# A decoder layer on one core: the setup loads issued from two queues in turns instead of one

## The chip, the cores and the metric

The kernel runs on one core of a Trainium2 chip. A core has five engines that this text names: PE (TensorE, matmuls and transposes), DVE (VectorE), ACT (ScalarE), POOL (GpSimd) and SP (SyncE, which computes nothing and issues transfers). Each engine works off its own list of instructions, in the order in which the program put them there. A DMA is issued by an instruction in the list of SP or of ACT; the bytes are then moved by 16 DMA engines. The metric is the device time of one execution in microseconds (us); lower is better.

## The reference

The reference is one pre-norm decoder layer in float32 over 128 sequences of 128 tokens with 256 features, 16 heads of 16 features. `_layernorm` has no weights.

```python
x = x + attn(_layernorm(x))                      # self attention, softmax over 128 keys, no mask
x = x + xattn(_layernorm(x), ctx_1024, mask)     # scores where mask == 0 are replaced by 1e-9
x = x + ffn(_layernorm(x))                       # 256 -> 1024 -> 256

def ffn(x):
    h = gelu(x @ absmean(W_fc).T)                # absmean: weights to -1, 0, 1
    return layernorm(h, ln_w, ln_b) @ absmean(W_proj).T

def absmean(W):
    Ws = W / (mean(abs(W)) + 1e-6)
    return sign(Ws) * minimum(round(abs(Ws)), 1)
```

The host only transposes the context and the weights.

## The kernel before, in words

The 128 sequences are worked in 32 groups of four (`G = 4`, 512 tokens). For each group a few streams of steps exist, written as Python generators: `prepare_self` (layer norm, transposes, queries, keys and values of self attention), `attention` (scores, softmax and weighted values of all rows), `prepare_keys` and `prepare_cross` (the same preparation for cross attention), `finish` (the feed-forward part). `constants` and `ternary_weights` run once. The order in which the streams advance is written out by hand: the strings `START`, `ORDER` and `END` hold one letter per step, and `for letter in START + ORDER * (n_groups - 4) + END: next(streams[letter])` (L859) emits the steps. Every engine's list follows that order. Nothing is reordered later; semaphore waits are added by the framework.

Ahead of all streams stands the setup block, L126 to L149. It is emitted first, so whatever it puts into an engine's list stands ahead of that engine's whole work. In this order it loads:

- the four sequences of group 0, `x`, 128 KB each, from SP and ACT in turns (L95), as loads 1 to 4;
- `attn_wq` (load 5), `attn_bq`, `attn_bk`, `attn_wk`, `attn_wv` (load 9), each weight 256 KB, each bias 1 KB, through `load` (L110);
- `ctx_t`, the context of group 0, 512 KB, through `load_context` (L102), load 10;
- `xattn_wk`, `xattn_wv` (loads 11 and 12), `xattn_bk`, `xattn_bq`, `attn_wo`, `attn_bv` (load 16) and `attn_bo`;
- the mask, `unmasked` (L136, load 18), and four copies of it in strips, `rows_32` (L140, loads 19 to 22);
- `xattn_wq`, `xattn_wo`, `xattn_bv`, `xattn_bo` (loads 23 to 26);
- the raw feed-forward weights `raw_w`, 1 MB each (L146, loads 27 and 28);
- `ln_w` and `ln_b` (loads 29 and 30), 4 KB each in 1024 separate elements of 4 bytes.

Only ACT's two loads of `x` are issued by ACT. All the others are issued by SP.

The first work after the setup block is the layer norm of group 0. `statistics` (L274) on DVE reads `x`, `deviation` (L280, L281) on POOL gives `rstd`, `apply` (L285) on DVE and POOL writes `xn`, PE transposes it into `pt` (L303), and ACT copies the two halves of `pt` to `xn_t` in `transposed_copy` (L314). These two copies are ACT's first instructions that compute. Then PE forms the queries `pq` (L323), and ACT writes `qt` from them (L380). `output_bias` (L218 to L221) uses `attn_bv` and `attn_wo`; `masks` (L223) reads the mask tiles; `ternary_weights` (L516) reads the raw weights.

Of the kernel before, what the change touches and what calls it, by code (L numbers as in the profile page):

```python
# [27 lines left out]
P = 128  # L28
# [9 lines left out]
S4 = 4  # L38
# [31 lines left out]
def tile_decoder_layer(ctx: ExitStack, tc: tile.TileContext, a: dict, out: bass.AP):  # L70
    nc = tc.nc
# [17 lines left out]
    def load_group(b):  # L89
        x = p_in.tile([P, G, D], F32, name="x", tag="x")  # L90

        queues = (nc.sync, nc.scalar) if b == 0 else (nc.sync,)
        step = G if b else 1
        for i, j in enumerate(range(0, G, step)):
            queues[i % len(queues)].dma_start(  # L95
                x[:, j : j + step], a["x"][b * G + j : b * G + j + step].rearrange("g s d -> s g d")
            )
        held[b] = x

    def load_context(b):  # L100
        ctx_t = p_in.tile([P, CC, T], F32, name="ctx_t", tag="ctx_t", bufs=1)
        nc.sync.dma_start(ctx_t, a["ctx_t"][:, b * T : (b + 1) * T].rearrange("(c p) t -> p c t", p=P))  # L102
        return ctx_t


    w_self, w_cross = {}, {}

    def load(name, shape, src):
        t = const.tile(shape, F32, name=name)
        nc.sync.dma_start(t, src)  # L110
        return t

    def load_weights(w, pre, names):
        for m in names:
            w[m] = load(f"{pre}_w{m}", [P, CC, D], a[f"{pre}_w{m}_t"].rearrange("(c p) o -> p c o", p=P))

    def load_biases(w, pre, names):
        for m in names:
            w["b" + m] = load(f"{pre}_b{m}", [P, CC], a[f"{pre}_b{m}"].rearrange("(c p) -> p c", p=P))

    def load_output(w, pre):
        load_weights(w, pre, "o")
        load_biases(w, pre, "v")
        w["bo"] = load(f"{pre}_bo", [P, D], a[f"{pre}_bo"][None, :].to_broadcast([P, D]))

    with nc.allow_non_contiguous_dma(reason="a few hundred bias elements, once"):  # L126
        load_group(0)
        load_weights(w_self, "attn", "q")
        load_biases(w_self, "attn", "qk")
        load_weights(w_self, "attn", "kv")  # L130
        context_0 = load_context(0)
        load_weights(w_cross, "xattn", "kv")
        load_biases(w_cross, "xattn", "kq")
        load_output(w_self, "attn")
        unmasked = p_one.tile([P, P], I32, name="unmasked", tag="xn_0")
        nc.sync.dma_start(unmasked, a["mask"])  # L136

        rows_32 = p_one.tile([P, S4, P], I32, name="rows_32", tag="xn_1")
        for r in range(S4):
            nc.sync.dma_start(rows_32[r * 32 : (r + 1) * 32], a["mask"].rearrange("(c i) k -> i c k", c=S4))  # L140
        load_weights(w_cross, "xattn", "q")
        load_output(w_cross, "xattn")
        raw_weights = []
        for src, shape in ((a["w_fc_t"], [P, CC, FF]), (a["w_proj_t"], [P, FC, D])):
            raw = p_one.tile(shape, F32, name="raw_w", tag="g", bufs=2)
            nc.sync.dma_start(raw, src.rearrange("(c p) o -> p c o", p=P))  # L146
            raw_weights.append(raw)
        ln_w = load("ln_w", [P, FC], a["ln_w"].rearrange("(c p) -> p c", p=P))
        ln_b = load("ln_b", [P, FC], a["ln_b"].rearrange("(c p) -> p c", p=P))  # L149
# [755 lines left out]
```

## Time and profile before

| | us |
|---|---|
| median of 3 runs (lowest, highest) | 2740.94 (2736.33, 2741.34) |
| the profiled execution, device time | 2737.08 |
| its span, from the first instruction to the last | 2735.1 |
| PE busy in the span | 2681.2 (98%) |
| ACT busy in the span | 1579.2 (58%) |

The profile is one execution, and its times count from the start of the span. An engine's row in the timeline gives the start, the length and, in square brackets, the idle time ahead of the instruction with what ended that idle time. "SPq" and "ACTq" are the issues of DMAs in the lists of SP and ACT: the length of such a row is how long the issuing engine was held, not how long the bytes travelled. The chain of waits is the work that ended last, followed back through what released each step. The trace also has a record of when the parts of each DMA had landed; the text calls these the completion records.

### The profile page before, as it was taken

The numbers are of one execution on the slowest core, as the hardware profiler recorded it, in microseconds if no ns is written. First come the engines' busy times: TensorE is split into PE (matmuls) and PEld (weight loads), VectorE is DVE, ScalarE is ACT, GpSimd is POOL, SyncE is SP. The second block draws the span as 40 slices with busy tenths as digits, with TensorE's granted clock in tenths as the row PEclk, the third lists the DMA queues.
The fourth block names the chain that finished last, engine by engine and source line by source line (L and its number), as shares of the span: only waits on it lengthen the run. The fifth ranks groups of instructions, "written<-read, shape, count | busy, mean of one in ns | idle before, by whom it ended". The sixth has DMA issues, their size and how long they took to land.

```text
span 2735.1 us, 77049 instructions
## 1 busy us (share of the span) xinstructions
PE 2681.2 (98%) x32845; PEld 1920.3 (70%) x32845; DVE 2118.4 (77%) x3916; ACT 1579.2 (58%) x2508; POOL 1336.5 (49%) x1425
## 2 busy tenths in 40 slices
PE   7999999999999999999999999999999999999998
PEld 4567777677777777776777776777777777777666
DVE  5677787777887777887777877777877778877777
ACT  3455665655665655666556666556656556665446
POOL 2344554544554554554445545445545445545443
PEclk9999999999999999999999999999999999999999
DMA  4121111221121221122211112211112211212210
GB/s 118 33 50 42 42 41 50 57 57 32 45 48 49 57 53 31 42 53 53 58 42 41 42 49 57 58 41 40 44 49 58 58 30 45 49 50 50 50 26 16
DMA packets 110093, 130.28 MB, mean 48 GB/s; under 512 B 32312, under 2 KB 69048, under 8 KB 109752
## 3 DMA queue, kind: packets, MB, share of 16 engines
q1 hardware_dynamic: 109464, 125.11, 18.9%
q8 instruction: 259, 4.24, 0.7%
q14 instruction: 82, 0.67, 0.1%
q10 hardware_dynamic: 288, 0.26, 0.0%
HBM read 71.38 MB, written 18.84 MB: 33 GB/s over the span
## 4 chain that ended last, share of the span: by engine, by line
PE 89%; DVE 7%; issue 2%; ACT 1%; POOL 1%; DMA 0%; DVEq 0%; POOLq 0%; ACTq 0%; SPq 0%
PE st L760 10%; PE av L805 9%; PE pq L323 9%; PE s L699 9%; PE py L500 8%; PE ph L442 8%; PE pk L323 8%; PE po L335 8%; PE pv L335 8%; PE pt L303 3%; PE pg L476 2%; PE s L688 2%; PE st L784 2%; DVE g L487 1%; PE pn L727 1%
## 5 line engine op out<-in xcount | busy, mean ns | idle before, releaser
L710 DVE TENSOR_REDUCE mx<-s 128x8 f32<-128x1024 f32 x512 | 601.0, 1215 | 83.7 <-PE s L699 83.2
L793 ACT ACTIVATE w_t<-st 128x1024 f32<-128x1024 f32 x512 | 496.8, 1022 | 202.6 <-PE st L784 122.0
L280 POOL TENSOR_SCALAR rstd<-agg 128x4 f32<-128x4 f32 (+2 forms) x163 | 39.0, 239 | 965.7 <-DVE agg L275 965.7
L285 POOL TENSOR_SCALAR xn<-x,agg,rstd 128x256 f32<-128x256 f32 x378 | 457.9, 1227 | 9.9
L413 POOL TENSOR_TENSOR o_raw<-o_raw,factors 128x256 f32<-128x256 f32 x252 | 181.4, 748 | 384.8 <-DMA factors<-by_head 279.3
L770 DVE COPY_PREDICATED_SCALAR st<-masked_t,masked_score 128x1024 f32 x256 | 316.1, 1280 | 68.3 <-PE st L760 68.3
L808 ACT COPY raw<-av 128x512 f32<-128x512 f32 x256 | 151.0, 590 | 318.7 <-PE av L805 313.8
L485 ACT ACTIVATE g<-pg,ln_w 128x256 fp32r<-128x256 f32 (+1 forms) x520 | 205.8, 473 | 175.8 <-PE pg L476 163.5
L699 PE MATMUL s<-kt,qt 32*128 32x256 f32 x4096 | 300.0, 403 | 3.2 <-ACT w_t L793 2.2
L500 PE MATMUL py<-w_proj,g 128*128 128x256 f32 x2048 | 279.8, 289 | 1.0 <-DVE g L487 0.6
L805 PE MATMUL av<-w_t,v 128*32 128x128 f32 x8192 | 279.4, 277 | 0.5 <-DVE q_max L732 0.4
L805 PEld LDWEIGHTS av<-w_t,v 128*32 128x32 f32 x8192 | 210.6, 110 | 98.4 <-issue 81.5
L500 PEld LDWEIGHTS py<-w_proj,g 128*128 128x128 f32 x2048 | 254.1, 189 | 12.9 <-issue 1.3
L442 PE MATMUL ph<-w_fc,xn 128*128 128x512 f32 x1024 | 259.4, 403 | 3.4 <-DVE v L371 1.2
L285 POOL TENSOR_SCALAR g<-g,agg,rstd 128x1024 f32<-128x1024 f32 x63 | 241.1, 3827 | 6.6
L487 DVE SCALAR_TENSOR_TENSOR g<-pg,ln_w,g 128x256 fp32r<-128x256 f32 (+1 forms) x520 | 212.5, 469 | 30.3 <-ACT g L485 30.0
L699 PEld LDWEIGHTS s<-kt,qt 32*128 32x128 f32 x4096 | 188.2, 185 | 63.8 <-issue 40.5
L442 PEld LDWEIGHTS ph<-w_fc,xn 128*128 128x128 f32 x1024 | 184.5, 188 | 58.1 <-DVE xn L431 10.3
L760 PEld LDWEIGHTS st<-q_max,kt 32*128 32x128 f32 x4096 | 128.7, 186 | 60.4 <-DVE negm_self L721 42.5
L274 DVE BATCH_NORM_STATS2 stats<-g 128x6 f32<-128x512 f32 x256 | 161.1, 670 | 1.0 <-ACT g L449 1.0
L449 ACT ACTIVATE g<-ph 128x512 f32<-128x512 f32 x256 | 146.6, 599 | 25.3 <-PE ph L442 24.1
L760 PEld LDWEIGHTS st<-qt,kt 32*128 32x128 f32 x4096 | 128.5, 186 | 45.4 <-DVE mx L710 25.0
(130 smaller groups left out, 4615.5 us busy)
## 6 DMA issues: line engine op xcount, KB each, us to landing
o_raw<-raw SPq DMA_DIRECT2D x504, 64.0 KB
factors<-by_head SPq DMA_DIRECT2D x126, 256.0 KB
ctx_t<-in_ctx_t_dram SPq DMA_DIRECT2D x32, 512.0 KB
x<-in_x_dram SPq DMA_DIRECT2D x31, 512.0 KB
out_dram<-x SPq DMA_DIRECT2D x31, 512.0 KB
sums<-raw SPq DMA_DIRECT2D x126, 16.0 KB
by_head<-r SPq DMA_DIRECT2D x63, 32.0 KB
raw_w<-in_w_fc_t_dram SPq DMA_DIRECT2D x1, 1024.0 KB
```

Of the source, the lines that this page charges most:

```text
L285: engine.tensor_scalar(dst[:, j], src[:, j], agg[:, j, 0:1], rstd[:, j : j + 1], ALU.subtract, ALU.mult)
L323: nc.tensor.matmul(out, w[:, c, o * P : (o + 1) * P], src_t[:, c], start=(c == 0), stop=(c == CC - 1))
L335: nc.tensor.matmul(rows[:, j], src_t[:, c, (j0 + j) * P : (j0 + j + 1) * P], w[:, c], start=(c == 0), stop=(c == CC - 1),)
L442: nc.tensor.matmul(ph, xn_parts[i][:, c, (j0 + j - at) * P : (j0 + j - at + 1) * P], w_fc[:, c, n * 512 : (n + 1) * 512], start=((i, c) == ...
L487: nc.vector.scalar_tensor_tensor(parts[1][:, f0 + f, tok], pieces[:, f], scales[f], parts[0][:, f0 + f, tok].bitcast(F32), ALU.mult, ALU.s ...
L500: nc.tensor.matmul(rows[:, j], parts[i][:, f, j * P : (j + 1) * P], w_proj[:, f], start=((i, f) == terms[0]), stop=((i, f) == terms[-1]),)
L699: nc.tensor.matmul(s[r // 2][:, r % 2, 2 * o : 2 * o + 2], qt[strip, o, tok], kt[strip, o, :, tok], start=(stage == "self"), stop=True, sk ...
L710: nc.vector.tensor_reduce(mx[:, 2 * half : 2 * half + 2], s[half], AX.X, ALU.max, negate=True)
L760: nc.tensor.matmul(s[r // 2][:, r % 2, n], kt[strip, n // 2, n % 2, tok], added[strip, n // 2, n % 2] if stage == "self" else qt[strip, n ...
L770: nc.vector.copy_predicated(s[half].rearrange("p r n q -> p (r n) q"), masked_t[:, None, :].to_broadcast([P, 8, P]), masked_score[:, :, No ...
L793: nc.scalar.activation(w_t[:, 2 * half : 2 * half + 2], s[half], AF.Exp)
L805: nc.tensor.matmul(av[32 * r : 32 * r + 32, n], v[:, j, head : head + 32], w_t[:, r, n], start=True, stop=True)
```

## The change

A helper `queue()` turns a list of two queues round at each call and returns the first: ACT at the first call, SP at the second, and so on. `load`, the load of the mask, the four strip loads and the two raw weight loads take their queue from it. The loads of `x` and of the context are as they were. The tiles, the order of the loads in the program and everything after the setup block are the same.

```diff
+    setup_queues = [nc.sync, nc.scalar]
+
+    def queue():
+
+        setup_queues.reverse()
+        return setup_queues[0]
+
     def load(name, shape, src):
         t = const.tile(shape, F32, name=name)
-        nc.sync.dma_start(t, src)
+        queue().dma_start(t, src)
         return t
...
-        nc.sync.dma_start(unmasked, a["mask"])
+        queue().dma_start(unmasked, a["mask"])
...
-            nc.sync.dma_start(rows_32[r * 32 : (r + 1) * 32], a["mask"].rearrange("(c i) k -> i c k", c=S4))
+            queue().dma_start(rows_32[r * 32 : (r + 1) * 32], a["mask"].rearrange("(c i) k -> i c k", c=S4))
...
-            nc.sync.dma_start(raw, src.rearrange("(c p) o -> p c o", p=P))
+            queue().dma_start(raw, src.rearrange("(c p) o -> p c o", p=P))
```

Counted through the program, ACT issues loads 2, 4, 5, 7, 9, 12, 14, 16, 18, 20, 22, 24, 26, 28 and 30, that is two of `x`, `attn_wq`, `attn_bk`, `attn_wv`, `xattn_wv`, `xattn_bq`, `attn_bv`, `unmasked`, the second and fourth strip, `xattn_wo`, `xattn_bo`, the raw projection weights and `ln_b`. SP issues the other fifteen.

## The prediction

> **What bounds the kernel now.** I read the page first: the shares by engine, then the chain that ended last.
>
> ```profile
> span 2735.1 us, 77049 instructions
> PE 2681.2 (98%) x32845; PEld 1920.3 (70%) x32845; DVE 2118.4 (77%) x3916; ACT 1579.2 (58%) x2508; POOL 1336.5 (49%) x1425
> PE 89%; DVE 7%; issue 2%; ACT 1%; POOL 1%; DMA 0%; DVEq 0%; POOLq 0%; ACTq 0%; SPq 0%
> ```
>
> PE is busy 98% of the span and carries 89% of the chain; DMAs carry 0%. So no steady part of the run waits for a load. Whatever the change does, it does in the first tens of microseconds, either by starting PE's stream earlier or by starting it later. The lists are fixed in order, so a shift of that start is carried to the end: nothing later on the chain is tied to the clock time of a setup load.
>
> Next the chain of waits in order of time, for the first 20 us:
>
> ```profile
> 0.72 2.66 DMA x<-in_x_dram
> ...
> 7.19 2.59 POOL xn L285 x2
> 9.78 0.04 issue
> 9.83 1.33 PE pt L303 x5
> 11.16 2.67 PE pq L323 x4
> 13.83 0.86 PE pb L220 x4
> 14.69 1.72 PE pq L323 x4
> 16.41 3.45 PE pk L323 x8
> ```
>
> The only load on it is `x`, which the change leaves alone. From 9.83 us the chain runs on PE without a break until 19.9 us, and through it passes ACT's copy of `pt` to `xn_t`. The timeline of ACT shows what stands in its list ahead of that copy:
>
> ```profile
> 0.72 0.90 ACTq L95 DMA_DIRECT2D x<-in_x_dram  x2
> 1.65 1.28 ACT L314 ACT_TABLE_LOAD   x1 [1.65 <-PEq L893]
> 10.34 0.59 ACT L314 COPY xn_t<-pt 128x512 f32<-128x512 f32 x1 [7.41 <-PE pt L303]
> 11.19 0.59 ACT L314 COPY xn_t<-pt 128x512 f32<-128x512 f32 x1 [0.27 <-PE pt L303]
> ```
>
> Two issues, a table load of 1.28 us that belongs to the copy's line and stands right ahead of it, and then 7.41 us idle. That idle time is all the cover that ACT can offer. Last, the timeline of SP, for what an issue holds the issuer, and SP's own waits:
>
> ```profile
> 8.25 0.47 SPq L110 DMA_DIRECT2D attn_bo<-in_attn_bo_dram  x1
> 10.46 0.34 SPq L136 DMA_DIRECT2D unmasked<-in_mask_dram  x1
> ...
> 15.67 0.47 SPq L146 DMA_DIRECT2D raw_w<-in_w_proj_t_dram  x1
> 16.18 2.60 SPq L110 DMA_DIRECT2D ln_w<-in_ln_w_dram  x1
> 18.83 5.20 SPq L110 DMA_DIRECT2D ln_b<-in_ln_b_dram  x1
> ```
>
> ```profile
> SPq L136 <- DMA ctx_t<-in_ctx_t_dram: 1.7, 1, 1.7
> SPq L140 <- DMA xattn_wk<-in_xattn_wk_t_dram: 0.4, 1, 0.4
> SPq L140 <- DMA xattn_wv<-in_xattn_wv_t_dram: 0.4, 1, 0.4
> ```
>
> The waits are the important lines. `unmasked` needs nothing of `ctx_t`, yet it waited for it; the first two strips waited for `xattn_wk` and `xattn_wv`. Counted through the program, load 18 waited for load 10, 19 for 11, 20 for 12: eight back each time. So the loads share eight completion semaphores in turn, over both queues, and every issue from load 9 on waits until the load eight places earlier has landed. On SP that held nobody. On ACT it would hold the copy at L314.
>
> **The change, part by part.** *What it takes from SP.* Thirteen issues leave SP's list. SP's next use is the `x` of group 1 (issued at 24.07), which DVE first reads at 36.77; after that SP's next issue is at 52.59. Neither is on the chain: worth 0. Bandwidth: the windows view has the DMA engines at a share of 0.78 in 0 to 10 us and 0.75 in 10 to 20 with one queue issuing, and no load but `x` on the chain, so faster landing is worth 0 as well. From below, could anything gain? The longest wait for a setup load, DVE for `attn_bv`, ends at 12.96, and PE only comes to that product (`pb`) at 13.66, directly behind `pq`. No gain.
>
> *What it puts on ACT.* Thirteen more issues, 15 in all, ahead of the table load and the two copies, since the setup block is emitted first. Issue alone costs 0.51 us from start to start (2.11, 2.62, 3.13, 3.65 on SP), so 15 of them end at 0.72 + 15 x 0.51 = 8.4 us if nothing holds them. With the table load, 9.7: still inside the idle time that ends at 10.34. What breaks the cover is the wait for eight back:
>
> - Load 18, `unmasked`, is now on ACT and waits for `ctx_t`. When does that land? Before, 1792 KB came with and ahead of it on one queue, and it landed at 10.45 (completion record; SP went on at 10.46). With two queues served in turns, SP has x, x, `attn_bq`, `attn_wk`, `ctx_t` (1025 KB) and ACT in as many descriptors x, x, `attn_wq`, `attn_bk`, `attn_wv` (769 KB): the same sum. I take 10.5, with 9.5 and 11.5 as bounds. ACT has issued nothing that computes by then.
> - Load 20 (second strip) waits for `xattn_wv`, before at 11.87: issued 11.9. Load 22 waits for `xattn_bq` (12.23): 12.3. Load 24 waits for `attn_bv` (DVE got it at 12.96): 12.9.
> - Load 26, `xattn_bo`, waits for `unmasked`, issued at 10.5. Before, that took from 10.46 to 13.68: 13.7.
> - Load 28, the raw projection weights, waits for load 20; the strip issued at 11.88 before landed at 14.08. ACT itself is free at 13.7 + 0.51. So 14.2.
> - Load 30, `ln_b`, waits for load 22 (landing about 14.3, 2.0 us after issue) and for ACT (14.7). Its own price is the open one. From below it is an ordinary issue, 0.47 us. From above it is `ln_b`'s 5.20. The nearest row is `ln_w`'s 2.60, which also followed the projection weights directly: from the issue of these to the end of `ln_w` it took 18.78 - 15.67 = 3.11 us. I take that: 14.2 + 3.11 = 17.3.
>
> Then the table load: 17.3 + 0.03 + 1.28, and the first copy starts at 18.6 instead of 10.34. Its input has been ready since 10.3. **The chain is late by 8.3 us.**
>
> *Behind the copy.* PE's list is at `pq`; DVE and POOL wait in turn for scores and rows; all of it moves together. Two small terms: the second copy then follows at once (0.5 us behind instead of 0.85), a gain of 0.3; and PE stands idle from about 11.2 to 19. The trace shows one slow stretch early on: the window 25 to 30 us, after PE had been idle, has a granted clock of 0.66, that is 3.4 us at half speed or 1.7 us lost. Whether the longer idle time adds such a stretch is open between 0 and 1.7; I take the middle, 0.8. Together +0.5, and the sum is **+8.8 us**.
>
> The profiled execution took 2737.08, its span 2735.1; the change would make that 2745.9. It lies below the median of the runs (2740.94), whose mean is 2739.5. I set the sum on the mean of the runs: 2739.5 + 8.8 = 2748.3.
>
> *Two rules held against rows.* The Trainium skill, "ScalarE: Activation LUTs", section "What ACT_TABLE_LOAD costs", gives 1283 ns for the load and about 1380 ns more for a drain. The row here has 1.28 us, and late in the run a table load that starts at 2720.57 is followed by an activation at 2721.86, so no drain shows; by the rule the estimate would be 1.4 us higher, 2749.7. The skill's "DMA: Bandwidth & Descriptors", section "Issuing engines are not separate DMA queues", says that issuing from several engines only saves sequencer time, "which is usually small relative to the DMA itself". The rows of 2.60 and 5.20 us for 4 KB speak against "small"; by the rule `ln_b` would cost an ordinary issue and the estimate would be 2746.2.
>
> **The rivals.** *`ln_b` finds room.* ACT's queue then holds only half the loads, so the issue may take 0.47 us: 14.7 + 0.04 + 0.47 = 15.2, copy at 16.5, late by 6.2 + 0.5 = 6.7, 2746.2. For it: less stands in each queue. Against: the 1024 pieces of the projection weights stand directly ahead in the same queue, as they did ahead of `ln_w`.
>
> *`ln_b` pays the full 5.20*, because the two queues hold each other up, or the strips land later: 2.6 more, 11.4 in all, 2750.9. For it: `ln_w` is issued from SP at the same moment. Against: nothing in this trace has two queues busy after 1.7 us.
>
> *ACT's idle time covers all of it; not slower.* If the alternating service brings the early loads home sooner, or the waits do not fall to ACT, its issues end at 8.4 and the table load at 9.7, and the copy starts at 10.34 as before: 2739.5. The point that decides is whether ACT's last issue ends before 9.0 us. Against: it would need `ctx_t` and the strips to land some five us earlier at an unchanged DMA share of 0.75 or more, and the eight-back waits are in the rows. For a real gain there is no place on the chain.
>
> **How the numbers follow.** Forecast 0.60; `ln_b` finds room 0.17; full price 0.15; covered 0.08. About 0.2%, 5.5 us here, is what a measurement of this kernel can tell from no change; against the median the line is at 2746.4. The forecast lies nearly all above it (0.56 of 0.60), the full price wholly (0.15), the cheap `ln_b` just under half (0.07): 0.78 slower. Of what is left, 0.19 is within the bound and 0.03 is faster, from run-to-run spread with the covered case. Range: the low end is the cheap `ln_b` with the runs' spread of 3 us below their mean, 2743; the high end is the full price with the top of the runs' spread and a whole slow stretch of PE (+1.9 and +0.9), 2754. That leaves the covered case and a little on each side outside.
>
> **What would show it.** Right: ACT's timeline has 15 issues, a gap at `unmasked` until about 10.5 us and waits for DMAs at the strips; the table load comes after the last issue, and the first copy starts near 18.6 without waiting for `pt`; the work of PE in the chain is unchanged, with a stretch ahead of it that is ACT's queue. SP's `x` of group 1 is issued several us before 24.07. Wrong: a first copy still at 10.3, a table load still at 1.65, or a copy at 18 us with a span that did not grow, which would mean that the early chain has slack I have not seen.

## The result, and the profile after

| | before | after |
|---|---|---|
| median, us (runs) | 2738.82 (9) | 2747.77 (9) |
| lowest to highest | 2733.58 to 2741.59 | 2743.42 to 2748.55 |
| profiled span | 2735.1 | 2744.9 |

The ratio is 1.0035, with a 95% interval of 1.0027 to 1.0044: slower by about 9 us. The forecast was 2748.3 us.

The page of the changed kernel, its span, the shares by engine and the chain:

```profile
span 2744.9 us, 77048 instructions
PE 2681.9 (98%) x32845; PEld 1920.5 (70%) x32845; DVE 2119.5 (77%) x3916; ACT 1579.1 (58%) x2508; POOL 1337.7 (49%) x1425
PE 89%; DVE 7%; issue 2%; ACT 1%; POOL 1%; DMA 1%; ACTq 0%; DVEq 0%; POOLq 0%; SPq 0%
```

All engines are busy for the same time as before, within 1.2 us (PE 2681.9 against 2681.2). The span grew by 9.8 us, so what was added is waiting. On the page only the DMA share of the chain shows it, 1% instead of 0%. ACT's timeline shows where it lies (an issue's row gives its start and how long ACT was held):

```profile
7.77 0.48 ACTq L143 DMA_DIRECT2D unmasked<-in_mask_dram  x1
9.33 2.35 ACTq L147 DMA_DIRECT2D rows<-in_mask_dram  x2
...
13.24 0.38 ACTq L153 DMA_DIRECT2D raw_w<-in_w_proj_t_dram  x1
16.88 0.38 ACTq L117 DMA_DIRECT2D ln_b<-in_ln_b_dram  x1
17.29 1.28 ACT L321 ACT_TABLE_LOAD   x1 [17.29 <-DMA xattn_bo<-in_xattn_bo_dram]
18.58 1.07 ACT L321 COPY xn_t<-pt 128x512 f32<-128x512 f32 x2
23.04 0.69 ACT L387 ACTIVATE qt<-pq,attn_bqs 128x512 f32<-128x512 f32 x1 [3.38 <-PE pq L330]
```

The first copy of `pt` starts at 18.58 us instead of 10.34, and no wait for PE stands beside it any more: its input had been ready for eight microseconds. The timeline of PE shows the same hole from the other side, 8.10 us idle ahead of `pq`, released by the copy (the last row is from the profile before, where `pq` followed the copy at once):

```profile
9.79 1.33 PE L310 MATMUL pt<-ident,xn 128*128 128x128 f32 x5 [0.52 <-POOL xn L292]
19.22 3.78 PE L330 MATMUL pq<-xn_t,attn_wq 128*128 128x512 f32 x4 [8.10 <-ACT xn_t L321]
```

```profile
10.98 2.85 PE L323 MATMUL pq<-xn_t,attn_wq 128*128 128x512 f32 x4
```

And the chain of waits of the first 19 us now runs through ACT's issues instead of through DVE, POOL and PE:

```profile
1.65 5.16 DMA attn_wq<-in_attn_wq_t_dram
...
7.25 4.79 DMA attn_bv<-in_attn_bv_dram
12.04 0.02 issue
12.06 0.42 ACTq L117
12.48 0.04 issue
12.52 4.76 DMA xattn_bo<-in_xattn_bo_dram
17.28 0.00 issue
17.29 0.11 ACT L321
```

One name in it has to be read with care. The table load is put down to `xattn_bo`, but by the completion records the last part of `xattn_bo` landed at 17.95, after the table load had begun. The table load started 0.03 us after the issue of `ln_b` had ended, when ACT's list came to it. What held `ln_b` is found by setting the starts of ACT's issues beside the completion records of the loads that had the same semaphore before them:

```
issue on ACT           start   the load it waited for     landed
attn_wv                 3.37   x, SP's first               3.34
xattn_wv                4.11   x, ACT's second             4.08
xattn_bq                6.84   attn_wq                     6.82
second strip            9.33   attn_wv                     9.31
fourth strip           11.36   xattn_wk                   11.34
xattn_wo               12.06   attn_bv                    12.04
raw projection weights 13.24   fourth strip               13.22
ln_b                   16.88   xattn_wo                   16.85
```

Each of these eight issues starts 0.02 or 0.03 us after the landing beside it. From 0.72 to 17.26 us ACT's list was held; the 15 issues took 6.24 us of that (the sum of their lengths), the gaps between them some 0.4, and the waits for landings about 9.9.

SP got its seven microseconds: the `x` of group 1 is issued at 17.07 instead of 24.07. No step of the chain of waits up to 45 us is a wait for that `x`.

### The profile page after: what moved, and what is told of

It reads as the page before. It is cut to its first block, busy times and chain, and to the rows that moved or that the text cites. A ratio compares the mean times of both kernels' runs of the same rounds, so it can differ in the third digit from the quotient of the medians.

```text
span 2744.9 us, 77048 instructions
## 1 busy us (share of the span) xinstructions
PE 2681.9 (98%) x32845; PEld 1920.5 (70%) x32845; DVE 2119.5 (77%) x3916; ACT 1579.1 (58%) x2508; POOL 1337.7 (49%) x1425
## 4 chain that ended last, share of the span: by engine, by line
PE 89%; DVE 7%; issue 2%; ACT 1%; POOL 1%; DMA 1%; ACTq 0%; DVEq 0%; POOLq 0%; SPq 0%
PE st L767 10%; PE av L812 9%; PE pq L330 9%; PE s L706 9%; PE ph L449 9%; PE pk L330 8%; PE py L507 8%; PE po L342 8%; PE pv L342 8%; PE pt L310 3%; PE pg L483 2%; PE s L695 2%; PE st L791 2%; DVE g L494 1%; DVE mx L717 1%
## 5 line engine op out<-in xcount | busy, mean ns | idle before, releaser
L706 PEld LDWEIGHTS s<-kt,qt 32*128 32x128 f32 x4096 | 188.6, 185 | 63.7 <-issue 40.1
```

The costliest lines, as they stand in the source:

```text
L706: nc.tensor.matmul(s[r // 2][:, r % 2, 2 * o : 2 * o + 2], qt[strip, o, tok], kt[strip, o, :, tok], start=(stage == "self"), stop=True, sk ...
```

## The experiments

Theory A, the forecast's: the first copy waits for its turn in ACT's list, and the run is late by as much as the copy is. Theory B: two queues bring the loads home later or in another order, and the layer waits for the loads. Ratios are against the kernel before, runs on the same chip.

**e1: only the early loads in turns** (loads 18 to 30 by SP):

```diff
+        setup_queues[:] = [nc.sync, nc.sync]
         unmasked = p_one.tile([P, P], I32, name="unmasked", tag="xn_0")
```

> The turns stop after load 17; loads 18 to 30 are issued by SP. Theory A (ACT's list holds its first copy): ACT has 8 issues, the last of them ended at 7.7 us in the changed kernel, so with 1.28 us of table load ACT is free by about 9.1 us, the first copy starts at 10.3 as before the change, and the time is that of before (within 1 us; ratio 1.000). Theory B (the loads land later or in another order when two queues carry them, and the layer waits for that): half or more of the 9 us stays, since the early loads, the ones that group 0 needs first, are split as in the changed kernel; ratio 1.002 to 1.0035.

Ratio 0.9999 (0.9991 to 1.0008). ACT's timeline:

```profile
7.26 0.48 ACTq L117 DMA_DIRECT2D attn_bv<-in_attn_bv_dram  x1
7.78 1.28 ACT L322 ACT_TABLE_LOAD   x1 [7.78 <-DMA attn_wv<-in_attn_wv_t_dram]
10.33 0.59 ACT L322 COPY xn_t<-pt 128x512 f32<-128x512 f32 x1 [1.27 <-PE pt L311]
```

And PE's:

```profile
10.97 3.78 PE L331 MATMUL pq<-xn_t,attn_wq 128*128 128x512 f32 x4
```

Eight issues and the table load end at 9.06, and the copy waits 1.27 us for PE as it should. The loads that group 0 needs are split over two queues here as in the changed kernel, and it costs nothing. That speaks for A and against B. (`pq` takes 3.78 us here too, although PE was not kept waiting; see the section on the prediction.)

**e2: only the late loads in turns** (the list starts as SP, SP and is set to the turns ahead of load 18):

```diff
-    setup_queues = [nc.sync, nc.scalar]
+    setup_queues = [nc.sync, nc.sync]
...
+        setup_queues[:] = [nc.sync, nc.scalar]
         unmasked = p_one.tile([P, P], I32, name="unmasked", tag="xn_0")
```

> SP issues loads 5 to 17, the turns begin with load 18. Theory A: ACT's last issue still waits for loads that land at 14 to 17 us, so it ends at 15 to 17.5 us, the first copy starts at 16.5 to 19, and the time is 6 to 9.5 us above before (ratio 1.0023 to 1.0035), although ACT has 9 issues instead of 15. Theory B: the early loads land as before the change, so at most 2 us (ratio below 1.0008).

Ratio 1.0040 (1.0027 to 1.0052). ACT's timeline:

```profile
6.22 0.35 ACTq L117 DMA_DIRECT2D xattn_bo<-in_xattn_bo_dram  x1
16.47 0.44 ACTq L154 DMA_DIRECT2D raw_w<-in_w_proj_t_dram  x1
16.95 0.64 ACTq L117 DMA_DIRECT2D ln_b<-in_ln_b_dram  x1
18.91 1.07 ACT L322 COPY xn_t<-pt 128x512 f32<-128x512 f32 x2
```

Nine issues cost as much as fifteen. Ten microseconds of ACT's list are one wait: the raw projection weights stand behind `attn_wo` on their semaphore, which landed at 16.45 by the completion records. (Unlike what B's expectation assumed, the early loads did not land as before: ACT's first late loads were issued early and ran beside them, and `attn_wv` landed at 12.68. So this run by itself does not refute B; e1 and e4 do.)

**e3: the last load back to SP.**

```diff
+        setup_queues[:] = [nc.sync, nc.sync]
         ln_b = load("ln_b", [P, FC], a["ln_b"].rearrange("(c p) -> p c", p=P))
```

> The changed kernel with its very last load, ln_b, issued by SP. Theory A: ACT's last issue is that of the raw projection weights, which ended at 13.6 us in the changed kernel; the table load follows, the first copy starts at about 14.9 instead of 18.6, and the time is 4.6 to 5.5 us above before (ratio 1.0017 to 1.002). So one load of 4 KB is worth 3.7 us. Theory B: all loads that group 0 needs are as in the changed kernel, so the time stays 9 us above before (ratio 1.0035).

Ratio 1.0027 (1.0018 to 1.0036), 7.4 us; the size that A expected (4.6 to 5.5 us) was missed. ACT's timeline:

```profile
13.39 0.50 ACTq L117 DMA_DIRECT2D xattn_bo<-in_xattn_bo_dram  x1
16.44 0.38 ACTq L153 DMA_DIRECT2D raw_w<-in_w_proj_t_dram  x1
16.85 1.28 ACT L322 ACT_TABLE_LOAD   x1 [16.85 <-DMA xattn_wo<-in_xattn_wo_t_dram]
18.15 1.07 ACT L322 COPY xn_t<-pt 128x512 f32<-128x512 f32 x2
```

The wait that was taken from the end of the list was replaced by the one ahead of it: the raw projection weights waited for the fourth strip, which landed at 16.42 here and at 13.22 in the profile of the changed kernel. The landings differ by 3 us, although each list holds the same issues in the same order up to there. What differs is the order between the lists: here SP issued `attn_bo` (128 KB) at 12.06, ahead of the strip at 12.31; in the changed kernel's profile it came behind it, at 11.61 against 11.36. In e6 and e9 below, which have the changed kernel's loads, `attn_bo` also came first, and the strip landed at 16.06 and 15.16. That this order makes the difference fits all four profiles, but no run isolates it. What the copy was late by, 7.81 us, still agrees with the time.

**e4: ACT held by computing, loads untouched** (the kernel before):

```diff
+    held_copy = values[1].rearrange("p j v -> p (j v)")[:, 0:1024]
+    nc.gpsimd.memset(held_copy, 0.0)
+    for _ in range(16):
+        nc.scalar.copy(held_copy, held_copy)
```

> The kernel before, all of its loads as they were, with 16 copies of 128x1024 in ACT's list ahead of its first real copy, which write a tile that is cleared later; nothing of the output changes. They should hold ACT until about 18.5 us. Theory A: the time rises by as much as in the changed kernel, 8 to 10 us if the first copy starts at 18.5 (ratio 1.003 to 1.0037), or else by the shift of that copy plus about 1 us. Theory B: no load is touched, so the time is that of before.

Ratio 1.0042 (1.0028 to 1.0056), that is 11.5 us. ACT's timeline:

```profile
3.67 17.19 ACT L195 COPY v<-v 128x1024 f32<-128x1024 f32 x16 [0.74 <-POOL v L193]
20.77 1.07 ACT L318 COPY xn_t<-pt 128x512 f32<-128x512 f32 x2
```

The copies took longer than planned and held ACT until 20.8: the first copy is 10.4 us late, the run about 11. Not a single load was moved. This is the effect of the change without the change, and B has no place for it.

**e5: the table load first** (one execution):

```diff
         load_group(0)
+        nc.scalar.preload_act_table(AF.Exp)
```

> The changed kernel with the table load placed right behind the two issues of x, ahead of ACT's other loads. Theory A (ACT's list holds its first copy, the table load included): the table load runs at 1.65 to 2.93, is hidden by the waits for landings behind it, and the first copy starts right behind the last issue: about 17.3 if the loads land as in the changed kernel, or in any case within 0.1 us of the end of the last issue instead of 1.3 us. Rival: the later issues all move by the 1.28 us, the last one too, and nothing is won (first copy at 18.6).

```profile
15.44 0.44 ACTq L117 DMA_DIRECT2D ln_b<-in_ln_b_dram  x1
15.92 1.07 ACT L322 COPY xn_t<-pt 128x512 f32<-128x512 f32 x2 [12.99 <-DMA xattn_bv<-in_xattn_bv_dram]
```

The copy starts 0.04 us behind the end of the last issue (15.88) instead of 1.32. So the table load's 1.28 us were part of the 8.24 and can be hidden. The last issue itself ended at 15.88 here instead of 17.26: with another order of the semaphores, `ln_b` stood behind the fourth strip, which landed at 15.42. The execution took 2741.94 us; a single execution does not tell what the hiding is worth, as e6 and e9 show.

**e6 and e9: PE kept busy in the hole.** 26 idle matmuls (nobody reads their result; the trace has two instructions for each) in the changed kernel, between the transposes of group 0 and `pq`:

```diff
+        if b == 0:
+            warm = bank("warm")
+            for _ in range(26):
+                nc.tensor.matmul(warm[:, 0:P], ident, ident, start=True, stop=True)
         unit = ready["self", b] = {}
```

> The changed kernel with 26 idle matmuls of 128x128 in PE's list between the transposes of group 0 and pq; they write a bank that nobody reads. They keep PE busy from about 11.2 to 18. If PE's slow start (pq 3.78 us instead of 2.85, pb 1.30 instead of 1.03) comes from the idle time that the change adds, pq takes 2.0 to 2.9 us here and qt follows the first copy by 3.5 us or less instead of 4.46. If it is only the phase of the clock in that execution, pq stays at 2.9 to 3.8.

> The same kernel as e6 (the changed kernel with idle matmuls on PE while ACT's list is held), now timed. In one execution it took 2739.9 us although its first copy started at 19.2. If the late copy still costs its 8.5 us and the idle matmuls win back only PE's slow start (1 to 2 us), the ratio is 1.0022 to 1.0030. If PE's slow stretches further on (23.7 us of granted half speed in the profile of the changed kernel, 8.7 in e6) really go away with them, up to 7 us come back and the ratio is 0.9995 to 1.0010.

PE's timeline in the single execution (e6), and then in the profile of the timed kernel (e9):

```profile
10.91 7.64 PE L571 MATMUL warm<-ident 128*128 128x128 f32 x52
19.83 1.99 PE L330 MATMUL pq<-xn_t,attn_wq 128*128 128x512 f32 x4 [1.28 <-ACT xn_t L321]
```

```profile
10.98 8.10 PE L571 MATMUL warm<-ident 128*128 128x128 f32 x52
18.91 1.88 PE L330 MATMUL pq<-xn_t,attn_wq 128*128 128x512 f32 x4
```

`pq` takes 1.9 to 2.0 us instead of 3.78. The single execution took 2739.89 us, as if the whole loss were gone; timed, the median is 2745.59 over 11 runs, ratio 1.0029 (1.0020 to 1.0038). Most of the loss stays, 7.9 us of it by this ratio; the one execution had been a lucky one. The windows view shows what was lucky in it. Its rows give the window and its length, the busy time of PE, PEld, DVE, ACT and POOL, then the granted clock of PE (the share of full speed that it was given), then the share of the DMA engines and GB/s; first e6, then e9:

```profile
20.00:110.00 90.00, 77.13 (x822) 48.49 (x822) 51.53 (x114) 35.80 (x50) 32.08 (x40) 0.98 0.17 39
```

```profile
20.00:110.00 90.00, 78.51 (x780) 49.53 (x779) 48.74 (x110) 33.16 (x45) 32.13 (x40) 0.91 0.17 39
```

It is the same program. By the trace's records of the clock, PE was at half speed for 6.8 us of e6's execution and for 23.9 us of e9's. An estimate from these: 17.1 us more at half speed are 8.5 us of lost work, and the two executions differ by 8.0 us (2739.89 and 2747.91). So the number of slow stretches varies between executions of one kernel, and that alone can hide the whole effect in a single execution.

**e7: late loads where ACT is idle.** As in e1, but loads 27 to 30 (raw weights, `ln_w`, `ln_b`) again in turns, put behind the `kt` copies of group 0:

```diff
+    def late_loads():
...
+            for engine, dst, src in (
+                (nc.sync, raw_weights[0], a["w_fc_t"].rearrange("(c p) o -> p c o", p=P)),
+                (nc.scalar, raw_weights[1], a["w_proj_t"].rearrange("(c p) o -> p c o", p=P)),
+                (nc.sync, ln_w, a["ln_w"].rearrange("(c p) -> p c", p=P)),
+                (nc.scalar, ln_b, a["ln_b"].rearrange("(c p) -> p c", p=P)),
+            ):
+                engine.dma_start(dst, src)
...
+        if late:
+            late.pop()()
```

> Turns up to load 17; loads 18 to 26 by SP; the raw weights, ln_w and ln_b (27 to 30) in turns again, but put into the lists behind the kt copies of group 0, where ACT had been idle from 21.3 to 30.9 us before. Theory A: ten loads on ACT then cost nothing, because each of ACT's issues lies where ACT would be idle anyway: ratio 1.000, within 0.1% of before. Theory B (two queues, or more loads on ACT, cost by themselves): ratio above 1.001.

Ratio 0.9997 (0.9988 to 1.0006). The same two loads that held ACT at 13.24 and 16.88 are now issued at 21.15 and 21.57, and nothing waits for ACT then:

```profile
21.15 0.37 ACTq L166 DMA_DIRECT2D raw_w<-in_w_proj_t_dram  x1
21.57 0.59 ACTq L166 DMA_DIRECT2D ln_b<-in_ln_b_dram  x1
30.95 1.94 ACT L813 ACTIVATE w_t<-st 128x1024 f32<-128x1024 f32 x2 [8.36 <-PE st L780]
```

With ten loads on ACT nothing is lost here, with nine in e2 all of it. So it is the place in the list that costs, not the number of loads on ACT.

**e8: GpSimd in ACT's place.**

```diff
-    setup_queues = [nc.sync, nc.scalar]
+    setup_queues = [nc.sync, nc.gpsimd]
```

> The changed kernel with GpSimd in the place of ACT in the turns. Theory A, taken over to another list: POOL's list now begins with 13 issues, which wait for landings in the same way, so that POOL's rstd of group 0, before at 5.7 us, starts behind the last of them, at 15 to 18 us, and everything behind it (xn, transposes, copies) moves by 9 to 12 us: ratio 1.0035 to 1.0050. The first copy of ACT is then late by waiting for pt, not by ACT's own list. Theory B: two queues cost the same whichever engine issues: about 1.0035, with rstd near 5.7.

Ratio 1.0041 (1.0026 to 1.0057). The timeline of POOL, the row of `rstd` in the kernel before, and the timeline of ACT:

```profile
12.66 0.88 POOL L117 DMA_DIRECT2D ln_b<-in_ln_b_dram  x1
13.53 0.22 POOL masks.py:197 MEMSET ident<- 128x128 f32 x1
17.12 0.23 POOL L287 TENSOR_SCALAR rstd<-agg 128x4 f32<-128x4 f32 x1 [1.55 <-DVE agg L282]
```

```profile
5.72 0.23 POOL L280 TENSOR_SCALAR rstd<-agg 128x4 f32<-128x4 f32 x1 [2.98 <-DVE agg L275]
```

```profile
21.75 0.59 ACT L321 COPY xn_t<-pt 128x512 f32<-128x512 f32 x1 [18.80 <-PE pt L310]
```

The delay moves with the list that is held: POOL's `rstd` starts at 17.12 instead of 5.72, and ACT now waits for PE. Between the last issue, which ends at 13.54, and `rstd` stands one more step: DVE's first instruction waits for `ident`, which POOL writes only then, and so DVE's statistics, which `rstd` needs, start at 14.82.

**e10 and e11: idle matmuls in the kernel before.** The hole in the changed kernel drew attention to PE's clock, so the kernel before got 22 idle matmuls ahead of its first transposes, and in e11 16 more in the hole ahead of the first matmul of `ternary_weights`:

```diff
+    warm = bank("warm")
+    for _ in range(22):
+        nc.tensor.matmul(warm[:, 0:P], ident, ident, start=True, stop=True)
...
+            total_bank = bank("total")
...
+            if raw is raw_weights[0]:
+                for _ in range(16):
+                    nc.tensor.matmul(total_bank[:, 0:P], ident, ident, start=True, stop=True)
```

> The kernel before, loads as they were, with 22 idle matmuls of 128x128 in PE's list ahead of the first transposes (about 1.3 to 7 us, where PE had nothing to do). If only the slow start counts, the first four pq take about 2.0 to 2.9 us and the whole gains 1 us at most: ratio 0.9995 to 1.000. If the slow stretches that follow depend on it, 4 to 7 us are won: 0.9975 to 0.9985.

> As e10, with 16 more idle matmuls ahead of the first matmul of ternary_weights, where PE was idle for 3.7 us and the clock then stood at half speed from 91.3 to 98.1 us. That stretch should go (3.4 us won at most, less the idle matmuls that do not fit into the gap): ratio 0.998 to 0.9995. If the clock's slow stretches do not follow PE's idle time, nothing changes against e10.

The first alone gives a ratio of 1.0000 (0.9991 to 1.0009): `pq` takes 1.98 us instead of 2.85, and that is within the noise. Both together give 0.9988 (0.9979 to 0.9997), median 2734.23 against 2736.85. The windows view from 85 to 100 us, first of the kernel before, then of e11:

```profile
85.00:100.00 15.00, 11.32 (x119) 6.43 (x113) 4.71 (x9) 3.82 (x5) 7.27 (x9) 0.77 0.01 2
```

```profile
85.00:100.00 15.00, 14.96 (x183) 11.16 (x176) 4.85 (x10) 6.61 (x10) 7.13 (x9) 1.00 0.01 3
```

The slow stretch after PE's 3.7 us of idle time is gone. In each of the other twelve profiles PE is idle for 2.6 to 3.7 us ahead of that matmul, and a stretch at half speed, 3.4 or 6.8 us long, begins within 2 us of the end of that idle time. But e11's profile has another stretch, of 3.4 us at 79.05 us, just ahead of this window, where the kernel before has none:

```profile
70.00:85.00 15.00, 13.88 (x159) 9.77 (x159) 12.40 (x29) 4.70 (x7) 8.77 (x11) 0.89 0.00 1
```

The gain of e11 is small and its interval ends close to 1; no run has the 16 matmuls without the 22. That the filled gap is what brought it is likely, not shown.

## Why the prediction was right, and which of its steps were not

**The mechanism** held: ACT's list, the waits for semaphores used before, the table load behind them. The first copy starts at 18.58; the sum had 18.6. By the profiles the first scores (`s`) are formed 9.40 us later than before, at 29.17 instead of 19.77: 8.24 of it is the copy's, 1.2 is that `pq` and `pb` took longer. The span grew by 9.8. Theory A's link from the copy to the time is shown from several sides: copies late by 0, 7.8, 8.2, 8.6 and 10.4 us went with ratios of 0.9999, 1.0027, 1.0035, 1.0040 and 1.0042.

**The steps that led to 17.3 did not hold one by one; two errors cancelled.** First, the partners of the waits. "Eight back through the program" fitted the rows of before, where one queue issued nearly all. With two queues the eight semaphores go round in another order: `unmasked` came behind `attn_bk` (landed at 7.59), not `ctx_t`, and was issued at 7.77 instead of 10.5. So the sign that the prediction named first, a gap at `unmasked` until 10.5, did not appear. Likewise the first of ACT's strips was issued at 9.33 instead of 11.9, and the raw projection weights at 13.24 instead of 14.2. That made the list about 1 us early. (The prediction's 1792 KB "on one queue" ahead of `ctx_t` included 256 KB from ACT's; no issue on ACT waited for `ctx_t` in the end.) Second, the price of `ln_b`. Its issue took 0.38 us, the rival's value, not the 2.60 of `ln_w`'s row. But it waited 3.26 us for `xattn_wo` (13.62 to 16.88), which landed 4.8 us after its issue; the sum had no such wait. From the issue of the projection weights to the end of `ln_b` it took 4.02 us, where the sum had 3.11. The end at 17.26 agrees with 17.3 by luck in these terms, and by the execution too: in e6 and e9, with the same loads, the issue of `ln_b` started at 17.49 and 16.39. What was sound in it: in these profiles and in e2 and e3 the last waits on ACT were for loads that landed between 16.3 and 17.5 us.

**The table load** cost its 1.28 us, as taken. The drain of about 1.4 us that the Trainium skill adds ("ScalarE: Activation LUTs", section "What ACT_TABLE_LOAD costs") does not show here either: the copy starts at 18.58, 0.01 after the load's end. The skill's other rule, that the sequencer time of an issue is usually small relative to the DMA itself ("DMA: Bandwidth & Descriptors", section "Issuing engines are not separate DMA queues"), agrees with `ln_b` here: its issue held ACT for 0.38 us, and its last part landed 8.7 us after the issue began. On SP, in the kernel before, it held the issuer for 5.20 us of the same 8.7, which is not small. And ACT's list was held mostly by the waits ahead of the issues, 9.9 us of 16.5, and of these the rule does not speak.

**PE's clock** was taken at +0.8, for a slow stretch that the longer idle time might add. The prediction saw one early stretch in the profile before; the records of the clock have three in the first 100 us, 3.4 us at 26.4 and at 40.1 and 6.8 us at 91.3. The changed kernel has two of 6.8 us, at 47.2 and 101.8. That is 13.7 us at half speed in both, and the windows view gives the same granted clock, first before, then after:

```profile
20.00:110.00 90.00, 78.33 (x877) 50.37 (x873) 54.83 (x115) 34.02 (x48) 29.32 (x36) 0.92 0.19 46
```

```profile
24.00:110.00 86.00, 74.25 (x768) 46.67 (x766) 49.51 (x110) 31.51 (x42) 32.11 (x40) 0.92 0.12 26
```

So these two executions show no added stretch; since e6 and e9 differ so much with one program, two executions do not settle what the change adds on average. What did differ is the start of PE's work. The records of the clock begin only at 12.76 us before and at 23.34 after, and up to there matmuls took longer than afterwards: the four matmuls of the first `pq` took 2.85 us before and 3.78 after, the next four 1.88 in both. With `pb` (1.03 and 1.30) that is the 1.2 us. But in e1 `pq` also took 3.78 with no added idle time, and the time was that of before. So the longer `pq` does not need the idle time; that the profile of before was a favourable execution is likely, but it is the only one kept of that kernel. Idle matmuls moved the ratio from 1.0035 to 1.0029 (e9, ahead of `pq`) and to 1.0000 (e10, ahead of the transposes, against 1 for the kernel before), which is no more than the intervals allow for noise. The gain of 0.3 for the second copy was not there to be had: in both profiles the second matmul of `pq` starts 1.0 us behind the first. The medians differ by 8.95 us, of which the profile's copy explains 8.24; the rest is not settled.

**No gain** from SP's side or from faster landing shows, as argued. **The covered case** was right in its condition, though not for this change: where ACT's last issue ended by 7.7 us (e1), the copy started at 10.33 and nothing was lost.

## What to carry to other kernels

Before moving a transfer to an engine that computes, look up in that engine's timeline how long it is idle ahead of its first work, and count the waits of the issues, not only the issues: in these kernels an issue that reused a semaphore held the whole list until an older load had landed. Put such issues behind the engine's urgent work, where it is idle anyway; in e7 they cost nothing that could be measured there (0.9988 to 1.0006). A sum that comes out right is no proof of its terms, so check the partner of each wait in the completion records. And a single execution is no timing: two of one kernel differed here by 8 us.

## What the runs showed that was not expected

With the same loads in each list up to it, the fourth strip landed anywhere between 13.22 us (the changed kernel's profile) and 16.42 (e3). PE's granted clock has slow stretches of 3.4 or 6.8 us early in the run. The one behind the idle gap at `ternary_weights` moves with the program, from 91.3 us before to 101.8 in the changed kernel; how many others there are varies between executions of one program. Filling that gap of 3.7 us with idle matmuls took the stretch behind it away, in the one profile that there is of it. And a single issue held GpSimd for longer than ACT: 0.55 to 0.96 us in e8 against 0.32 to 0.51 in the changed kernel's profile (at most 0.71 on ACT, in e3).
